# Performer layer and eight-expert MLP on one core: the eighth expert's bias added to its rows before the products, the seventh's rows finished tile by tile, and three tiles' logit steps of the last batch on GpSimd

## The chip, the cores and the metric

One Trainium2 chip, one core. The metric is the device time of one execution of the whole program in microseconds (us), given as the median of several runs. The engines are named as the profile names them: PE is TensorE (matmuls), PEld its weight loads, DVE is VectorE, ACT is ScalarE, POOL is GpSimd, SP is SyncE, which only issues DMAs. PSUM is the memory that matmuls write to, SBUF the memory that all engines read and write.

## The reference, cut to what matters

The input is 8 x 512 tokens of 256 numbers. Each token passes a layer of linear attention with an MLP, then a mixture of 8 experts. In the second part each expert takes the 512 tokens with the highest gate score for it (so a token can have several experts, or none), and adds its weighted output to those tokens.

```python
def ffn(x):                       # x: 4096 rows of 256
    scores = softmax(x @ gate_w.T)            # 8 experts
    vals, idx = top_k(scores.T, 512)          # for each expert: its 512 rows
    y = layernorm(x[idx]) * ln_w + ln_b
    h = gelu(y @ fc1s[e] + b1s[e])            # 1024 hidden
    out = (h @ fc2s[e] + b2s[e]) * vals       # bias b2s, then the weight
    return x.at[idx].add(out)                 # added to the rows

x = x + layernorm(attention_layer(layernorm(x)))
x = x + layernorm(ffn(layernorm(x)))
```

All is float32. A token's result is final when every expert that chose it has added its output; then the row is normalised once more, added to the row that the first part gave (the residual), and written to the output.

## The kernel before, in words

**Two stages with a search between them.** The first stage runs over 8 batches of 512 tokens, each of 4 tiles of 128 tokens (one token per partition). It computes attention and MLP, three layernorms one after the other (letters c, d and e in the code) and, beside them, the gate logits. The logits aren't computed from the finished row: they are carried along as 8 extra columns of the tile `r1x` (columns D to D + E), and each layernorm's effect on them is made up for by small steps on 8 numbers per token: subtract the mean times a constant row, multiply by the root, add another row. `share` (line 486) does this on VectorE, one tile at a time, in one operation or two (L488, L490); `shares` (line 471) does it on GpSimd, in two operations or four (L478, L479, L481, L482). In batches 0 to 6 GpSimd does it for all four tiles at once. In the last batch (`last_mlp`, line 1155) VectorE does it tile by tile, inside the steps `second`, `third` and `fourth` of each tile (lines 1261 to 1281).

The square root of a layernorm, `root` (line 156), is on GpSimd: add epsilon (L157), raise to -0.5 (L158). So each tile of the last batch goes VectorE, GpSimd, VectorE, GpSimd, and so on: step 1 on VectorE (task `("L", b, t, 1)`: take the MLP's product out of PSUM, L1254; mean and variance, `stats`, L153 and L154; first half of the affine map, L1258), root 1 on GpSimd (`("R", b, t, 1)`), step 2 on VectorE (L183, `stats`, L180 for the centring), root 2, step 3 (L183, `stats`), root 3, step 4 (the bias of the last normalisation, L1278).

When all four tiles' logits are done, `chosen_from` (line 1022) turns them into scores: largest value (L1026), difference (L1028), times the root (L1031), all on VectorE, then the exponential on ScalarE (L1035), then sum, reciprocal and product on VectorE (L1038 to L1041). These are the tasks `("CH", b, 0)` to `("CH", b, 2)`. The search needs the scores of the whole input: about 30 rounds of compare and count on VectorE and TensorE (L1477 to L1489), then the row numbers of each expert, its gather of rows (`y`, L1612) and its first product.

**The experts.** For each expert e (0 to 7; the text's "eighth" is e = 7) there are 4 tiles j of 128 rows. TensorE computes the hidden part (`hidden`, L1717) and the second product (`weighted`, L1735), which stays in PSUM. ScalarE takes it out and multiplies it by the token's score (`weighted_out`, L1743, task `We`), VectorE adds the bias times the score (`with_bias`, L1750, task `WB`). For e < 7 GpSimd then issues a DMA that adds the rows to a table in DRAM (`scatter`, L1626, with an addition; task `A1` for the table `accs`). From e = 3 (`L0`) on, the rows' final value is made along the way: before expert e adds, its 512 rows of `accs`, sum and residual, are gathered into `zg` (`gather_sum`, L1612, task `Q`), VectorE adds the expert's own output there (`sum_rows`, L1784, task `U`), takes mean and variance (`told`, task `RS`), GpSimd the root (`RR`), VectorE normalises and adds the residual, and GpSimd scatters the rows to the output (task `P`, L1626 without addition). A later expert that has some of the same tokens writes them again, so the scatters of expert e follow those of e - 1. For e = 3 to 6 mean, root, normalisation and residual are done for the four tiles together: `told` for 4, one `root` on 4 columns, four `applied` (L161), one `with_residual` over 1024 columns (L1775), and only then the four scatters. For e = 7 they are done tile by tile: `RS`, `RR`, and `finish_row` (L161 through `plain`, then L1790).

**What sets the order.** Each engine works through its own queue in program order, and the program order is made on the host by a planner (line 187). Every piece of work is a task with an engine, a cost, a place and the tasks that it must follow. The planner keeps a clock for each engine; it takes, for the engine that can start first, the task with the lowest place among those that can start by then (within 0.05). So costs and places change the order of instructions in a queue, and nothing else: a task with a low place goes ahead of others only if the planner thinks that it is ready. The places of the first stage get 66 for each batch. Those of the experts get 31 for each expert (`SPAN`), through the local function `task` (line 1796). The tasks with a DMA behind them (gathers, scatters, weight loads) are added by `landed` (line 1664), which calls the planner's `add` directly with the place that it is given.

GpSimd's queue holds, in the expert stage, the roots, all gathers and all scatters; each gather or scatter holds the engine for 1.0 to 1.7 us while it makes the descriptors (L1612, L1626), and each scatter has a tiny memset ahead of it (L1625).

## Time and profile before

| | us |
|---|---|
| median of 3 runs | 895.32 (892.78 to 896.16) |
| profiled execution, its own time | 894.79 |
| its span, first to last instruction | 893.1 |
| TensorE busy | 787.7 (88%) |
| VectorE busy | 594.5 (67%) |
| ScalarE busy | 352.6 (39%) |
| GpSimd busy | 344.8 (39%) |
| last matmul of the last batch (L1242) ends | 579.7 |
| exponential of the last batch's scores (L1035) starts | 590.72 |
| first gather of the experts (L1612) starts | 633.64 |
| last product of the eighth expert taken out of PSUM (L1743) starts | 875.82 |
| last scatter (L1626) starts | 885.00 |

How to read it: the span is counted from the first instruction, and all times below are positions on it. Busy shares are means over stages that differ: TensorE is nearly idle from 580 to 638 and after 876, and without rest between. A line of the timeline gives start, duration, engine, source line, operation, what it writes and reads, and in brackets how long the engine was idle before it and which instruction's end released it.

### The profile page before, as it was taken

What the parts mean: (1) busy time and instruction counts of PE and PEld (TensorE: products, weight loads), DVE (VectorE), ACT (ScalarE), POOL (GpSimd) and SP (SyncE); (2) the same over time, 40 slices, a digit from 0 to 9 for tenths busy, and PEclk for the clock granted to TensorE, in tenths of its full rate; (3) what the DMA queues carried; (4) which work ended last, traced back from release to release, by engine and by line L of the source; (5) the groups of instructions that cost most, each with busy time, mean ns of one, the idle gap of its engine ahead of it and who ended that gap; (6) DMA issues with size and microseconds to landing.
All of it is one profiled execution on the core that took longest, in us unless ns stands there. A gap on an engine that the chain in (4) does not pass through costs nothing.

```text
span 893.1 us, 14823 instructions
## 1 busy us (share of the span) xinstructions
PE 787.7 (88%) x5620; PEld 552.1 (62%) x5620; DVE 594.5 (67%) x1631; ACT 352.6 (39%) x638; POOL 344.8 (39%) x548
## 2 busy tenths in 40 slices
PE   4998899999999989999989999911599999999992
PEld 2675585575586666576577578801385676667761
DVE  4568658688677788787877876887553112977223
ACT  3461624454464364463464463300233223322230
POOL 5077103313203213302312302640156766766775
PEclk9998999999999999999999999955599999999996
DMA  9000001301300400400210300174036659987541
GB/s 309 2 2 1 1 1 36 107 3 43 100 1 1 142 3 1 142 2 2 93 51 1 119 2 1 48 241 184 25 103 147 123 116 324 268 284 226 161 95 47
DMA packets 62231, 79.46 MB, mean 89 GB/s; under 512 B 8016, under 2 KB 52304, under 8 KB 62032
## 3 DMA queue, kind: packets, MB, share of 16 engines
q1 hardware_dynamic: 51600, 60.18, 20.3%
q0 software_dynamic: 9856, 17.46, 8.9%
q8 instruction: 44, 0.72, 0.3%
q10 hardware_dynamic: 704, 0.88, 0.3%
q14 instruction: 27, 0.22, 0.1%
HBM read 45.33 MB, written 33.18 MB: 88 GB/s over the span
## 4 chain that ended last, share of the span: by engine, by line
PE 44%; DVE 23%; POOL 12%; issue 12%; DMA 7%; ACT 2%; POOLq 0%; SPq 0%; ACTq 0%; DVEq 0%
PE pm L1004 7%; PE ph L951 6%; PE ptq L833 3%; PE pc L744 3%; PE pv L688 3%; DMA z<-acc 3%; POOL accs L1626 2%; PE pw L932 2%; PE pk L564 2%; PE pq L564 2%; DVE qd L814 2%; DVE sh L807 2%; PE phe L1717 2%; PE pdiv L864 2%; PE pxk L627 2%
## 5 line engine op out<-in xcount | busy, mean ns | idle before, releaser
L951 PE MATMUL ph<-xaT,w_sb 128*128 128x512 f32 (+1 forms) x288 | 118.3, 553 | 0.4 <-ACT hT L956 0.4
L1717 PE MATMUL phe<-yT,w1e 128*128 128x512 f32 (+1 forms) x288 | 115.2, 555 | 0.2 <-ACT yT L1707 0.2
L1735 PE MATMUL pwe<-w2e,hTe 128*128 128x256 f32 x512 | 112.7, 380 | 0.0
L1004 PE MATMUL pm<-w_sb,hT 128*128 128x264 f32 x448 | 107.6, 389 | 0.0
L1735 PEld LDWEIGHTS pwe<-w2e,hTe 128*128 128x128 f32 x512 | 96.5, 190 | 13.5 <-issue 0.5
L1004 PEld LDWEIGHTS pm<-w_sb,hT 128*128 128x128 f32 x448 | 82.3, 190 | 15.5 <-issue 2.8
L1717 PEld LDWEIGHTS phe<-yT,w1e 128*128 128x128 f32 x288 | 54.9, 194 | 51.8 <-issue 48.8
L951 PEld LDWEIGHTS ph<-xaT,w_sb 128*128 128x128 f32 x288 | 53.4, 191 | 48.1 <-issue 36.6
L956 ACT ACTIVATE hT<-ph,cols_sb 128x512 f32<-128x512 f32 (+1 forms) x72 | 45.7, 637 | 68.3 <-PE ph L951 68.3
L1726 ACT ACTIVATE hTe<-phe,cols_sb 128x512 f32<-128x512 f32 (+1 forms) x72 | 45.9, 640 | 66.8 <-PE phe L1717 65.7
L724 ACT ACTIVATE kp<-kp,nstab 128x256 f32<-128x256 f32 x128 | 53.5, 495 | 32.8 <-DVE nstab L677 32.8
L1612 POOL DMA_INDIRECT y<-xg,idx x32 | 33.8, 1056 | 68.3 <-DVE idx L1609 40.0
L1626 POOL DMA_INDIRECT accs<-o,idx x28 | 47.1, 1681 | 16.1 <-issue 10.1
L646 DVE TENSOR_REDUCE mxk<-pxk 128x8 f32<-128x512 f32 x64 | 43.7, 683 | 7.0 <-PE pxk L627 7.0
L1743 ACT ACTIVATE o<-pwe,gg 128x256 f32<-128x256 f32 x32 | 15.1, 473 | 83.7 <-PE pwe L1735 73.0
L807 DVE TENSOR_REDUCE sh<-pxq 128x8 f32<-128x512 f32 x64 | 40.9, 681 | 9.8 <-PE pxq L627 9.7
L814 DVE TENSOR_TENSOR qd<-pxq,sh 128x512 f32<-128x512 f32 x64 | 43.0, 687 | 2.6 <-PE ptq L833 0.5
L649 DVE TENSOR_TENSOR kp<-pxk,diag 128x512 f32<-128x512 f32 x64 | 43.7, 683 | 0.0
L844 ACT ACTIVATE qpT<-ptq 128x512 f32<-128x512 f32 x64 | 35.1, 595 | 19.7 <-PE ptq L833 19.4
L744 PE MATMUL pc<-kp,v_aug 128*34 128x128 f32 x512 | 36.9, 294 | 5.7 <-DVE kp L730 5.7
L833 PE MATMUL ptq<-ident,qd 128*128 128x128 f32 x256 | 35.4, 278 | 5.1 <-ACT qd L826 4.3
L157 POOL TENSOR_SCALAR rs_b<-mv_b 128x4 f32<-128x4 f32 (+1 forms) x9 | 2.4, 269 | 91.9 <-DVE mv_b L154 91.9
(273 smaller groups left out, 1525.0 us busy)
## 6 DMA issues: line engine op xcount, KB each, us to landing
w1e<-in_f SPq DMA_DIRECT2D x8, 1024.0 KB, 6.4
w2e<-in_f SPq DMA_DIRECT2D x8, 1024.0 KB, 8.9
z<-acc SPq DMA_DIRECT2D x8, 1024.0 KB
x<-in_x_in SPq DMA_DIRECT2D x8, 512.0 KB, 9.3
accs<-x SPq DMA_DIRECT2D x8, 512.0 KB, 3.1
acc<-x SPq DMA_DIRECT2D x8, 512.0 KB, 4.3
xg<-xf SPq DMA_DIRECT2D x8, 512.0 KB, 4.3
accs<-xf SPq DMA_DIRECT2D x8, 512.0 KB, 4.2
```

What stands on the lines that cost most here:

```text
L724: nc.scalar.activation(kp[:, :, h, :], kp[:, :, h, :], AF.Exp, bias=nstab[:, h : h + 1])
L744: nc.tensor.matmul(pc[s * 64 : s * 64 + 2 * (DH + 1), i, :], v_aug[:, t, pair, :].rearrange("p h d -> p (h d)"), kp[:, t, pair, :].rearran ...
L807: nc.vector.tensor_reduce(head_cols(kept["sh", b, t], i), pxs[:, :, i, :, :], AX.X, ALU.max,)
L814: nc.vector.tensor_tensor(heads(get("qd", u), c), pxs[:, :, c, :, :], head_cols(kept["sh", b, t], c) .unsqueeze(3).to_broadcast([P, 4, 2, M]),
L833: nc.tensor.transpose(pt[:, i, :], get("qd", u)[:, 2 * hp : 2 * hp + 2, :].rearrange("p h m -> p (h m)"), ident,)
L951: nc.tensor.matmul(ph, w1_sb[:, c, ts(f, P)], get("xaT", b)[:, c, cols], start=(c == 0), stop=(c == KD - 1),)
L956: nc.scalar.activation(get("hT", b)[:, f, cols], ph, AF.Relu, bias=cols_sb[:, C_B1 + f : C_B1 + f + 1])
L1004: nc.tensor.matmul(kept["PM", b, t, 0], get("hT", b)[:, f, ts(t, P)], w2_sb[:, f, :], start=(f == 0), stop=(f == NF - 1),)
L1626: this = nc.gpsimd.indirect_dma_start(out=table[:, :], out_offset=bass.IndirectOffsetOnAxis(ap=idxs[e][:, j : j + 1], axis=0), in_=src, in ...
L1717: nc.tensor.matmul(ph, w1e[:, c, ts(f, P)], yT[:, c, cols], start=(c == 0), stop=(c == KD - 1))
L1726: nc.scalar.activation(hTs[e][:, f, cols], kept["H", e, f, i], AF.Gelu_apprx_tanh, bias=cols_sb[:, col : col + 1],)
L1735: nc.tensor.matmul(kept["W", e, j], hTs[e][:, f, ts(j, P)], ws[e][1][:, f, :], start=(f == 0), stop=(f == NF - 1),)
```

## The change

It has three parts.

1. **Eighth expert.** ScalarE's pass over the product and VectorE's `with_bias` are left out for e = 7. The bias times the score is added to the gathered rows as soon as they are there (`bias_to_rows`, task `UB`), and the product goes from PSUM, times the score, into the same rows in one VectorE operation (`last_sum`, task `U`).
2. **Seventh expert.** The four `applied` and the one `with_residual` become four `finish_row`, one for each tile, and each tile's scatter follows its own row. The places of mean, root, rows and scatters are lower. The cost that the planner is given for the eighth's roots goes from 0.8 to 1.6.
3. **Last batch.** For tiles 0 to 2 the logit steps leave VectorE's steps and become tasks of their own on GpSimd (`LG`), by `shares` on one tile; those of tile 2 are told to follow roots of tile 3. For the last tile they stay on VectorE, and its last one moves from step 4 into step 3. `chosen_from` is cut once more, between the difference and the product with the root, so that largest value and difference wait for the logits only.

```diff
-        def chosen_from(b, pl, rs):
+        def chosen_from(b, pl, rs, early=False):
...
+            if early:
+                yield
             nc.vector.tensor_tensor(
                 ex, ex, rs.unsqueeze(2).to_broadcast([P, NT, E]), ALU.mult
             )
...
+            def to_logits(t, letter, i, plus=None):
+                (mv, rs), x = one(letter, t), in_r1(b)
+                if t == NT - 1:
+                    share(x[:, t, :], mv[:, 0, 0:1], i, rs if plus is not None else None, plus)
+                else:
...
+                    shares(
+                        nc.gpsimd, x[:, t : t + 1, :], mv[:, :, 0], i,
+                        rs if plus is not None else None, plus,
+                    )
+            def logits_2(t):
+                to_logits(t, "c", ns3, k3)
+            def logits_3(t):
+                to_logits(t, "d", ns1, note("x0g", b, None)[:, t, :])
+            def logits_4(t):
+                to_logits(t, "e", ns1)
...
-                    share(in_r1(b)[:, t, :], one("c", t)[0][:, 0, 0:1], ns3, one("c", t)[1], k3)
+                    if t == NT - 1:
+                        logits_2(t)
...
-                    share(
-                        in_r1(b)[:, t, :], one("d", t)[0][:, 0, 0:1], ns1, one("d", t)[1],
-                        note("x0g", b, None)[:, t, :],
-                    )
+                    if t == NT - 1:
+                        logits_3(t)
+                        logits_4(t)
...
-                    share(in_r1(b)[:, t, :], mv[:, 0, 0:1], ns1)
...
-                    (1, 1.48, first, "c"), (2, 1.75, second, "d"), (3, 1.4, third, "e"),
-                    (4, 0.34, fourth, None),
+                    (1, 1.48, first, "c"), (2, 1.75 if last else 1.3, second, "d"),
+                    (3, 1.65 if last else 1.1, third, "e"), (4, 0.16, fourth, None),
...
+                if not last:
+                    for step, weight, work in (
+                        (2, 1.0, logits_2), (3, 1.0, logits_3), (4, 0.5, logits_4)
+                    ):
+                        task(
+                            ("LG", b, t, step), "POOL", weight, at_ + 6 + 2.5 * step,
+                            lambda t=t, work=work: work(t),
+                            [("L", b, t, step - 1)]
+                            + ([("R", b, t, step - 1)] if step < 4 else [])
+                            + ([("LG", b, t, step - 1)] if step > 2 else [])
+                            + ([("R", b, t + 1, min(step - 1, 2))] if t == NT - 2 else []),
+                        )
...
-            for i, (engine, weight) in enumerate((("DVE", 0.57), ("ACT", 0.23), ("DVE", 0.53))):
...
+                (("DVE", 0.38), ("DVE", 0.19), ("ACT", 0.23), ("DVE", 0.53))
...
+                    ("CH", b, i), engine, weight, 82 + 0.1 * i, lambda i=i: chosen(i),
+                    [("CH", b, i - 1)] + ([("R", b, t, 3) for t in range(NT)] if i == 1 else [])
+                    if i else [("LG", b, t, 4) for t in range(NT - 1)] + [("L", b, NT - 1, 3)],
...
+    def bias_to_rows(e, j):
+        zj = zgs[e][:, j, 0:D]
+        nc.vector.scalar_tensor_tensor(
+            zj, b2s_sb[:, e, :], ggs[e][:, j : j + 1], zj, ALU.mult, ALU.add
+        )
+
+    def last_sum(e, j):
+        zj = zgs[e][:, j, 0:D]
+        nc.vector.scalar_tensor_tensor(
+            zj, kept["W", e, j], ggs[e][:, j : j + 1], zj, ALU.mult, ALU.add
+        )
...
+            if e == E - 1:
+                continue
             task(
                 ("We", e, j), "ACT", 0.48, 18.7 + 3.6 * j, lambda e=e, j=j: weighted_out(e, j),
...
+                task(
+                    ("UB", e, j), "DVE", 0.49, 10 + 3.6 * j, lambda e=e, j=j: bias_to_rows(e, j),
+                    [("Q", e, j), ("K", e)],
+                )
+                task(
+                    ("U", e, j), "DVE", 0.49, 18.7 + 3.6 * j, lambda e=e, j=j: last_sum(e, j),
+                    [("UB", e, j), ("W", e, j, 1)], back=("W", e, j, 0),
+                )
...
-                    ("RR", e, j), "POOL", 0.8, 21.5 + 3.6 * j,
+                    ("RR", e, j), "POOL", 1.6, 21.5 + 3.6 * j,
...
-            late = 32 if e < E - 2 else 31
+            late = 32 if e < E - 2 else 26
...
+            if e == E - 2:
+                for j in J:
+                    task(
+                        ("RX", e, j), "DVE", 0.84, late + 3.5 + 0.5 * j,
+                        lambda e=e, j=j: finish_row(e, j), [("RW", e)],
+                    )
...
-                ("P", e, j), "POOL", 1.4, ((late + 10) if e < E - 1 else 25) + 2 * j,
+                ("P", e, j), "POOL", 1.4, ((late + (10 if e < E - 2 else 4)) if e < E - 1 else 25) + 2 * j,
                 lambda e=e, j=j: scatter(out, e, j, zgs[e][:, j, 0:D]),
-                [("RX", e, j) if e == E - 1 else ("RX", e)]
+                [("RX", e, j) if e >= E - 2 else ("RX", e)]
```

## The prediction

> **What bounds the kernel now.** I read the busy shares of the page first, then busy time by stage (the windows view), then the chain of waits, then the two ends that the change touches, row by row on the timeline. In the windows view the columns are stage, length, then each engine's busy time, granted clock, DMA share and GB/s.
>
> ```profile
> 563.00:577.00 14.00, 14.00 (x65) 11.99 (x64) 13.10 (x48) 4.87 (x10) 6.20 (x13) 1.00 0.21 72
> 577.00:592.00 15.00, 2.91 (x14) 2.20 (x14) 11.87 (x47) 3.62 (x8) 11.55 (x27) 0.66 0.50 166
> 640.00:860.00 220.00, 220.00 (x1030) 150.54 (x1031) 103.50 (x274) 71.29 (x123) 144.59 (x170) 0.99 0.67 182
> 876.00:886.00 10.00, 0.00 (x0) 0.00 (x0) 6.08 (x16) 0.30 (x1) 6.71 (x14) 0.64 0.11 39
> ```
>
> From 640 to 860 TensorE is busy all 220.00 us and nothing in the change touches it. The change can act in two places: the end of the last batch (577 to 592), where VectorE and GpSimd hand a chain to and fro while TensorE idles, and the tail after the last product (876 on). Whatever the first place wins passes whole to the end: from the scores on, the chain is the search on VectorE (592 to 633), then the gathers, then the unbroken TensorE stretch. The first place ends like this:
>
> ```profile
> 587.57 0.48 DVE L183 SCALAR_TENSOR_TENSOR x<-r1x,rs_d,x 128x256 f32<-128x256 f32 x1
> ...
> 588.81 0.22 POOL L157 TENSOR_SCALAR rs_e<-mv_e 128x1 f32<-128x1 f32 x1 [0.70 <-DVE mv_e L154]
> ...
> 589.12 0.57 POOL L158 TENSOR_TENSOR rs_e<-rs_e,mhalf 128x1 f32<-128x1 f32 x1
> ...
> 589.72 0.16 DVE L1278 SCALAR_TENSOR_TENSOR nbe<-mv_e,rs_e 128x1 f32<-128x1 f32 x1 [0.62 <-POOL rs_e L158]
> ...
> 590.50 0.19 DVE L1031 TENSOR_TENSOR ex<-ex,rs_e 128x32 f32<-128x32 f32 x1
> ...
> 590.72 0.23 ACT L1035 ACTIVATE ex<-ex 128x32 f32<-128x32 f32 x1 [0.20 <-DVE ex L1031]
> ```
>
> The last root ends at 589.69; five small VectorE steps stand between it and the exponential at 590.72. The tail, GpSimd and the VectorE steps that it waits for:
>
> ```profile
> 864.51 1.01 POOL L1612 DMA_INDIRECT zg<-accs,idx  x1 [0.30 <-issue]
> ...
> 865.89 1.04 POOL L158 TENSOR_TENSOR rs_r<-rs_r,mhalf 128x4 f32<-128x4 f32 x1
> ...
> 866.97 1.38 DVE L161 TENSOR_SCALAR zg<-zg,mv_r,rs_r 128x256 f32<-128x256 f32 x4 [15.11 <-POOL rs_r L158]
> 868.38 1.23 DVE L1775 TENSOR_TENSOR zg<-zg 128x1024 f32<-128x1024 f32 x1
> ...
> 869.90 1.11 POOL L1626 DMA_INDIRECT out<-zg,idx  x1 [2.91 <-DVE zg L1775]
> ...
> 873.96 0.97 POOL L1626 DMA_INDIRECT out<-zg,idx  x1 [0.22 <-issue]
> 874.96 0.26 POOL L157 TENSOR_SCALAR rs_r<-mv_r 128x1 f32<-128x1 f32 x1
> ...
> 881.77 1.09 POOL L1626 DMA_INDIRECT out<-zg,idx  x1 [1.14 <-DVE zg L1790]
> ...
> 885.00 1.09 POOL L1626 DMA_INDIRECT out<-zg,idx  x1 [1.15 <-DVE zg L1790]
> ```
>
> From 865 GpSimd's queue sets the end, not the products: the root of the seventh expert, a wait of 2.91 for its rows, its four scatters, and only then the roots of the eighth (874.96), though the first products were ready at 865.4. After the last scatter (886.09) comes only its landing, to 893.1.
>
> **The tail, part by part.** I call the experts 6 and 7, as the code does. Does the root of expert 6 move ahead of the gathers, as its earlier place (26 for 31) might suggest? Its mean was ready at 851.86 and it still ran at 865.55. The reason is in the code: names added through `landed` carry no offset of their expert, so gathers and scatters have places from -24 to 48, while a root of expert 6 has 186 + 28 = 214. A ready scatter or gather always wins. So the order stays: scatters of 5, gathers of 7, root of 6 at 865.55. What changes is what follows. Rows leave tile by tile: scale 0.41 and residual 0.43 (L161, L1790) with a gap of 0.04 end at 866.97 + 0.88 = 867.85, in place of 869.61; the scatter starts 0.29 later, as now: 868.14 for 869.90, **1.76 earlier**. The other three follow at GpSimd's pace (4.06 for the three), slower than VectorE's 0.88 a tile.
>
> Expert 7's bias step (0.48) moves ahead of the products and the ACT pass (0.47), bias (0.48) and add (0.42) become one operation from PSUM; no row has that form, the nearest are 0.43 (L1254, PSUM and SBUF) and 0.48 (L1750): 0.45, and between 0.4 and 0.6 nothing hangs on it. It frees about 0.9 us of latency per tile. What hides that is GpSimd: by hand through the new order on VectorE the four means are ready at 872.6, 873.8, 877.1 and 880.4, and GpSimd comes to their roots at 873.2, 874.1, 877.9 and 881.1. From the first root on GpSimd's string (root, root, scatter, scatter, root, scatter, root, scatter; places 25 to 31 for the scatters, 238 and more for the roots) is the one of now, with its waits for root, row and scatter; it ran from 874.96 to 885.00 and starts 1.76 earlier. Were that cover gone, the last tile alone would give 875.8 + 0.5 + 0.6 + 0.95 + 0.9 + 0.3 = 879.1. **The tail: -1.76.** New waits: the bias steps of tiles 0 and 1 stand on VectorE ahead of the rows of 6 and wait for the gathers of 7, the second of which is issued by 862.89, 4.08 before VectorE is wanted.
>
> **The last batch.** VectorE loses, for three tiles, small steps of 0.40, 0.37 and 0.14 by their pitch (L488, L490), 2.7 us in all; the last tile keeps them. GpSimd gains, per tile, two steps of four operations and one of two, on 128x8. No row has 8 wide. Nearest: 128x16, shortest 0.21, gap 0.08: 4 x 0.29 = 1.16. Above: the means of the 32-wide rows, 0.34 + 0.38 + 0.31 + 0.41 and four gaps, 1.76, waits within the operations included. I take 1.35, nearer the narrow one (two operations: 0.62, ends 0.58 and 0.88). A root of one tile takes 0.88 where undisturbed (579.16 to 580.04) and 1.05 on the mean of the twelve: 0.95.
>
> Then the order by the planner's rule (first ready, among those the lowest place). With the added steps GpSimd no longer rests: from the second root of tile 0 (ready 566.6, as now) I find no wait over 0.2 down to the last root. In order: that root, step 2 of tile 0's logits, root 1 of tile 1, root 3 of tile 0, and so on; batch 6's root, its logits and its rescale; then roots of tiles 2 and 3 with tile 2's steps among them, and the last step and batch 6's copy ahead of the last root. The sum: 11 roots x 0.95 = 10.45; 5 four-operation steps x 1.35 = 6.75; 3 of two x 0.62 = 1.86; batch 6: root 1.33, logits 0.71, rescale 2.02, copy 0.42, 4.48. Together 23.54, so the last root ends at 590.15, **0.46 later** than now. VectorE falls out as the bound: its stretch to 576.89 ends about 1.7 sooner, and the last product (579.66) now waits for nobody. Behind the root stand no longer five steps but one: largest value and difference move ahead of it, so the exponential starts 0.06 + 0.20 + 0.03 = 0.29 after it in place of 1.03: 590.44 for 590.72. **-0.3.** Ends of this term: roots 0.89 and steps 1.16 / 0.58 with 0.3 of waits for VectorE give 589.0, -1.7; roots 1.05 and steps 1.76 / 0.88 give 566.6 + 27.5 + 0.29 = 594.4, +3.7.
>
> The waits within GpSimd's operations can be seen:
>
> ```profile
> 583.11 0.48 DVE L1258 SCALAR_TENSOR_TENSOR r1x<-r1x,mv_c,rows_sb 128x256 f32<-128x256 f32 x1
> 583.16 0.51 POOL L157 TENSOR_SCALAR rs_c<-mv_c 128x1 f32<-128x1 f32 x1 [0.23 <-DVE mv_c L154]
> ```
>
> The same GpSimd operation took 0.22 at 582.06, beside a VectorE add that reads PSUM (581.97); here it ends 0.08 after the VectorE step does. The Trainium skill ("SBUF — State Buffer", section "SBUF: two separate sides") says why: the two engines share a pair of ports, a VectorE operation with two SBUF inputs takes it whole against a GpSimd operation that reads SBUF, and who starts second waits. It speaks against moving small steps to GpSimd; the row agrees. By that rule alone, each step caught once (+0.29), the string would be 8 x 0.29 = 2.3 longer than undisturbed steps; by no lock, 1.16 a step.
>
> **The sum.** -0.3 - 1.76 = -2.0 on the profiled execution's 894.79 (span 893.1): **892.8 us**. It lies 0.5 below the median of the runs shown (895.32).
>
> **Rivals.**
> 1. GpSimd's string in the last batch stretches (the slower side). Place: between 566.6 and the last root; price up to +3.7, so 894.79 + 3.7 - 1.8 = 896.7. It decides once the string is 2.0 longer than 23.54, that is a four-operation step of 1.67. For it: no rest is left in the queue, and 0.22 became 0.51 above. Against it: VectorE has less to do there. The Trainium skill's rule of the shared port (same page and section) is this rival's mechanism. Chance 0.2.
> 2. The planner gives GpSimd the last root ahead of the third scatter of expert 7. Then the root's 0.9 and the wait for the rows lie beside the scatter: last scatter at 881.4, the tail -3.6; with the undisturbed steps 894.79 - 1.7 - 3.6 = 889.5, with mine 890.9. For it: the eighth's rows are ready sooner. Against: that scatter's place is 29, and it is ready as soon as its row is. Chance 0.15, of which 0.1 below 890.3.
> 3. The bias steps at the head of VectorE's queue hold back the rows of 6: it takes a gather's landing of over 4.08 (a gather of y landed in 2.85, a scatter with addition in up to 6.73). At 6.73 the rows start 3.1 later, tail +1.4: 895.9. Chance 0.05.
> 4. The change does nothing that counts: string and tail as now, 894.8. Chance 0.05.
>
> The forecast has 0.51 (its own range 891.3 to 894.5); 0.04 is left for what I have not seen. The range that should hold the time 8 times in 10: **890.6 to 896.0**. About 0.5% (4.5 us) is what a measurement of this kernel can tell from no change. Faster by more: 0.1 (rival 2). Slower by more needs 899.3, beyond every end above: the 0.04 left over. Within: 0.86.
>
> **What would show it.** In the profile after: the root of expert 6 behind the four gathers of 7, its first scatter 1.2 after that root's end (2.97 now), the eighth's first root right behind the fourth scatter; the gap from first root to last scatter unchanged at 10.04. In the last batch: GpSimd without rests of over 0.3 from 567 on, the exponential 0.3 behind the last root. Wrong would be: roots of 7 waiting for means rather than for GpSimd, rests on GpSimd before the last root, or the last root before 589.

## The result, and the profile after

| | before | after |
|---|---|---|
| median of 9 runs each, side by side | 895.32 (892.78 to 899.20) | 890.64 (887.87 to 892.04) |
| profiled execution, its own time / span | 894.79 / 893.1 | 887.87 / 886.2 |

The ratio is 0.9942, 95% interval [0.9926, 0.9959]. By this ratio the change saves 5.2 us (the two medians are 4.7 apart), where 2.0 were forecast. The sign and the tail were right, the size was not.

The two profiles are 6.9 us apart, but not all of that is the change. The second root of the last batch's first tile starts at 566.64 before and at 564.50 after, so 2.14 us lay between the two executions already. (The first moved step runs ahead of it, in time in which GpSimd was idle before; the tile's first root, ahead of every moved step, lies 2.16 apart.) I therefore compare stretches, each from its own start:

| us | before | after | difference |
|---|---|---|---|
| second root of tile 0 to the end of the last root | 23.05 | 21.92 | -1.13 |
| last root's end to the exponential | 1.03 | 0.29 | -0.74 |
| exponential to the experts' first gather | 42.92 | 42.61 | -0.31 |
| expert 6's first scatter into `accs` to the last scatter | 37.30 | 35.65 | -1.65 |
| sum | | | -3.83 |

The 0.95 still missing to 6.9 lies in TensorE's unbroken stretch, from the first gather to that scatter into `accs` (214.06 before, 213.11 after).

The windows of after, with the columns of before (stage, length, PE, PEld, DVE, ACT, POOL, granted clock, DMA share, GB/s):

```profile
563.00:577.00 14.00, 14.00 (x66) 12.03 (x65) 11.78 (x39) 5.89 (x13) 11.07 (x37) 1.00 0.23 77
577.00:592.00 15.00, 1.69 (x8) 0.90 (x7) 12.30 (x50) 2.47 (x7) 12.07 (x31) 0.59 0.68 219
640.00:855.00 215.00, 215.00 (x1014) 146.63 (x1013) 100.18 (x267) 68.19 (x117) 144.13 (x170) 1.00 0.69 186
871.00:880.00 9.00, 0.00 (x0) 0.00 (x0) 3.39 (x10) 0.00 (x0) 5.44 (x11) 0.62 0.16 55
```

In the first row GpSimd has gone from 13 operations and 6.20 to 37 and 11.07, VectorE from 48 to 39 operations; part of that is that after runs 2.14 ahead in the same window. The third row is TensorE's unbroken work, as before. Now GpSimd's timeline in the last batch; an operation's share of the queue is read from its start to the next start:

```profile
564.50 0.39 POOL L157 TENSOR_SCALAR rs_d<-mv_d 128x1 f32<-128x1 f32 x1 [0.70 <-DVE mv_d L154]
...
568.57 0.20 POOL L478 TENSOR_TENSOR gm<-mv_c,gk 128x8 f32<-128x8 f32 x1
568.85 0.20 POOL L479 TENSOR_TENSOR r1x<-r1x,gm 128x8 f32<-128x8 f32 x1
569.13 0.20 POOL L481 TENSOR_TENSOR r1x<-r1x,rs_c 128x8 f32<-128x8 f32 x1
569.41 0.28 POOL L482 TENSOR_TENSOR r1x<-r1x,gk 128x8 f32<-128x8 f32 x1
569.65 0.20 POOL L478 TENSOR_TENSOR gm<-mv_e,gk 128x8 f32<-128x8 f32 x1
569.93 0.20 POOL L479 TENSOR_TENSOR r1x<-r1x,gm 128x8 f32<-128x8 f32 x1
570.10 0.22 POOL L157 TENSOR_SCALAR rs_d<-mv_d 128x1 f32<-128x1 f32 x1
...
572.47 0.22 POOL L157 TENSOR_SCALAR rs_e<-mv_e 128x1 f32<-128x1 f32 x1 [0.43 <-DVE mv_e L154]
...
585.85 0.57 POOL L158 TENSOR_TENSOR rs_e<-rs_e,mhalf 128x1 f32<-128x1 f32 x1
```

A step of four takes 1.08 (568.57 to 569.65), one of two 0.45 (569.65 to 570.10), and the only idle time over 0.3 from there up to the last root is the 0.43 at 572.47 (the next longest is 0.14). The end of the batch over all engines:

```profile
585.97 0.18 DVE L1026 TENSOR_REDUCE lm<-r1x 128x4 f32<-128x32 f32 x1
...
586.19 0.19 DVE L1028 TENSOR_TENSOR ex<-r1x,lm 128x32 f32<-128x32 f32 x1
...
586.48 0.19 DVE L1033 TENSOR_TENSOR ex<-ex,rs_e 128x32 f32<-128x32 f32 x1
...
586.71 0.23 ACT L1037 ACTIVATE ex<-ex 128x32 f32<-128x32 f32 x1
```

The last root ends at 586.42. Largest value and difference run beside it (585.97, 586.19), and one product (L1033, L1031 before) stands between root and exponential. GpSimd in the tail:

```profile
859.22 1.01 POOL L1647 DMA_INDIRECT zg<-accs,idx  x1 [0.31 <-issue]
...
860.76 1.04 POOL L158 TENSOR_TENSOR rs_r<-rs_r,mhalf 128x4 f32<-128x4 f32 x1
...
863.00 1.11 POOL L1661 DMA_INDIRECT out<-zg,idx  x1 [1.14 <-DVE zg L1838]
...
868.07 0.25 POOL L157 TENSOR_SCALAR rs_r<-mv_r 128x1 f32<-128x1 f32 x1
...
874.86 1.09 POOL L1661 DMA_INDIRECT out<-zg,idx  x1 [1.15 <-DVE zg L1838]
...
878.08 1.09 POOL L1661 DMA_INDIRECT out<-zg,idx  x1 [1.15 <-DVE zg L1838]
```

The wait ahead of expert 6's first scatter is 1.14 instead of 2.91; behind it stands the order of before, and from 868.07 to 878.08 it takes 10.01 (10.04 before).

### The profile page after: what moved, and what is told of

Read it like the earlier page. It is cut to its first block, busy times and chain, and to the rows that moved or that the text cites. A ratio compares the mean times of both kernels' runs of the same rounds, so it can differ in the third digit from the quotient of the medians.

```text
span 886.2 us, 14834 instructions
## 1 busy us (share of the span) xinstructions
PE 787.3 (89%) x5620; PEld 552.6 (62%) x5620; DVE 595.1 (67%) x1619; ACT 351.0 (40%) x634; POOL 350.2 (40%) x578
## 4 chain that ended last, share of the span: by engine, by line
PE 68%; DVE 16%; POOL 5%; issue 5%; ACT 3%; DMA 1%; POOLq 0%; ACTq 0%; DVEq 0%
PE phe L1752 11%; PE pwe L1770 11%; PE ph L951 7%; PE pm L1004 7%; PE pc L744 4%; PE ptq L833 3%; PE pv L688 3%; PE pw L932 3%; PE pk L564 2%; PE pq L564 2%; PE pxq L627 2%; PE pdiv L864 2%; PE pxk L627 2%; PE pr L909 2%; PE pm L1262 2%
## 5 line engine op out<-in xcount | busy, mean ns | idle before, releaser
L814 DVE TENSOR_TENSOR qd<-pxq,sh 128x512 f32<-128x512 f32 x64 | 42.9, 686 | 2.6 <-PE ptq L833 0.5
L1778 ACT ACTIVATE o<-pwe,gg 128x256 f32<-128x256 f32 x28 | 13.3, 474 | 75.2 <-PE pwe L1770 75.2
```

## The experiments

Two theories stood against each other. **S**: the sum stands and only the size of GpSimd's string in the last batch was wrong; what is left over separates executions of one kernel. **M**: another stretch, above all the one from the scores to the experts, gains by itself. All ratios are to the kernel before, run beside on the same chip. In the table, "string" runs from the second root of tile 0 to the end of the last root, "behind" from there to the exponential, "search" from the exponential to the experts' first gather, "rows and scatters" from expert 6's first scatter into the output to the last scatter, "tail" from expert 6's first scatter into `accs` to the last scatter.

| | ratio, interval | string | behind | search | rows and scatters | tail |
|---|---|---|---|---|---|---|
| before | 1 | 23.05 | 1.03 | 42.92 | 15.10 | 37.30 |
| after | 0.9942 [0.9926, 0.9959] | 21.92 | 0.29 | 42.61 | 15.08 | 35.65 |
| e1_batch_only | 0.9975 [0.9961, 0.9990] | 21.84 | 0.29 | 42.59 | 15.09 | 37.26 |
| e2_tail_only | 0.9971 [0.9952, 0.9989] | 23.04 | 1.04 | 42.89 | 15.08 | 35.71 |
| e3_rows_only | 1.0008 [0.9988, 1.0027] | 23.03 | 1.03 | 42.89 | 17.29 | 37.69 |
| e4_product_only | 0.9984 [0.9969, 1.0000] | 23.04 | 1.03 | 42.89 | 14.11 | 36.64 |
| e5_split_only | 1.0014 [0.9994, 1.0033] | 23.05 | 0.44 | 43.26 | as before | 37.31 |
| e6_gpsimd_only | 1.0006 [0.9987, 1.0026] | 21.69 | 1.04 | 42.93 | as before | 37.26 |
| e7_two_more | 0.9989 [0.9969, 1.0010] | 23.96 | 0.26 | 42.59 | as after | 35.55 |
| e8_late_rescale | 0.9913 [0.9894, 0.9932] | 21.60 | 0.29 | 43.04 | as after | 35.76 |
| e9_tail_order | 0.9957 [0.9936, 0.9978] | 21.82 | 0.30 | 42.61 | 16.53 | 36.34 |
| e10_both_orders | 0.9967 [0.9952, 0.9982] | 21.74 | 0.29 | 43.06 | 16.41 | 36.21 |
| e11_before_again | 0.9987 [0.9971, 1.0004] | 23.06 | 1.04 | 42.93 | as before | 37.31 |
| e12_products_first | 0.9937 [0.9915, 0.9959] | 21.85 | 0.30 | 42.61 | 13.49 | 33.34 |
| e13_changed_again | 0.9967 [0.9952, 0.9981] | 21.83 | 0.30 | 42.61 | as after | 35.84 |
| e14_late_rescale_again | 0.9967 [0.9953, 0.9980] | 21.75 | 0.29 | 43.04 | as after | 35.71 |

**The two halves.** The change to the last batch alone, and the two parts of the tail alone.

```diff
 # e1_batch_only, against the kernel before: part 3 of the change
+            if early:
+                yield
...
+            def to_logits(t, letter, i, plus=None):
...
+                            ("LG", b, t, step), "POOL", weight, at_ + 6 + 2.5 * step,
```

> Only the last batch's part of the change; the tail is that of before. In the two profiles the exponential of the scores comes 1.85 us sooner when counted from batch 6's first third-normalisation row (561.88 and 559.72), not 0.3 as forecast. Theory S (the sum stands, the GpSimd string was sized too long, and the rest of the gap between the two profiles is chance of the execution): about -1.9 us, ratio 0.998. Theory M (the stretch from the scores to the experts adds a gain of its own, 0.6 in the first matmuls of the first expert and some 0.6 around them): about -3.1 us, ratio 0.9965. In the profile both expect the last root to end about 22 us behind the start of the second root of tile 0 and the exponential 0.29 behind the last root; S expects the first eight matmuls of expert 0 to take 3.1 or 3.7 without regard to the change.

```diff
 # e2_tail_only, against the kernel before: parts 1 and 2 of the change
+                    ("UB", e, j), "DVE", 0.49, 10 + 3.6 * j, lambda e=e, j=j: bias_to_rows(e, j),
...
+                        ("RX", e, j), "DVE", 0.84, late + 3.5 + 0.5 * j,
```

> Only the two expert parts of the change; the last batch is that of before. Theory S: -1.65 us, ratio 0.998, first scatter of the seventh expert's rows 1.2 behind the root's end (2.97 before), and 15.1 from that first scatter to the last, as before. Rival P (the eighth's product leaving by one operation is worth time by itself): more than -1.65, and less than 15.1 between the two scatters.

The last batch alone gives 0.9975, the tail alone 0.9971; their stretches are each as in the whole change (21.84 and 0.29; 35.71), and the rest of each as before. The interval of the first ratio holds what both theories expect (0.998 and 0.9965), so it's the stretches that speak for S. The product of the two ratios is 0.9946, against 0.9942 measured. So there are two parts that add, and no third that needs both has to be assumed. Half of the win, about 2 us, comes from the last batch, which had been forecast at 0.3.

**The tail in its parts.** Only the seventh expert's rows by tile, and only the eighth's products by one operation (with its cost for the planner).

```diff
 # e3_rows_only, against the kernel before
-            late = 32 if e < E - 2 else 31
+            late = 32 if e < E - 2 else 26
...
+                        ("RX", e, j), "DVE", 0.84, late + 3.5 + 0.5 * j,
+                        lambda e=e, j=j: finish_row(e, j), [("RW", e)],
```

> Only the seventh expert's rows by tile, with its new places; the eighth expert is that of before, its roots' planner cost is 0.8 again. The planner now orders GpSimd root 0, scatter 0, root 1, scatter 1, root 2, scatter 2, root 3, scatter 3. Theory S (GpSimd's order and length set the tail): the first scatter of the seventh comes 1.76 sooner, but root 1 stands behind scatter 0, which waits for root and row, so most is given back: about -0.2 us. A theory by which only the seventh's rows matter expects -1.7.

```diff
 # e4_product_only, against the kernel before
+                    ("U", e, j), "DVE", 0.49, 18.7 + 3.6 * j, lambda e=e, j=j: last_sum(e, j),
+                    [("UB", e, j), ("W", e, j, 1)], back=("W", e, j, 0),
...
-                    ("RR", e, j), "POOL", 0.8, 21.5 + 3.6 * j,
+                    ("RR", e, j), "POOL", 1.6, 21.5 + 3.6 * j,
```

> Only the eighth expert's part (bias first, product by one operation, its roots' planner cost 1.6); the seventh's rows are those of before. GpSimd's order becomes root 0, root 1, scatter 0, root 2, scatter 1, scatter 2, root 3, scatter 3. Theory S: the seventh's first scatter stays (2.97 behind the root), root 2 ahead of scatter 1 saves one wait: about -0.9 us. Rival P: -1.5 or more. A theory by which the eighth's part is worth nothing: 0.

With the rows alone, the first scatter is 1.76 earlier (1.21 behind the root's end, 2.97 before), and all of it is given back: rows and scatters take 17.29. GpSimd's timeline of that kernel shows how:

```profile
874.68 1.34 POOL L1626 DMA_INDIRECT out<-zg,idx  x1 [1.34 <-DVE o L1750]
876.05 0.24 POOL L157 TENSOR_SCALAR rs_r<-mv_r 128x1 f32<-128x1 f32 x1
...
878.15 1.09 POOL L1626 DMA_INDIRECT out<-zg,idx  x1 [1.15 <-DVE zg L1790]
...
881.36 1.09 POOL L1626 DMA_INDIRECT out<-zg,idx  x1 [1.15 <-DVE zg L1790]
...
884.58 1.09 POOL L1626 DMA_INDIRECT out<-zg,idx  x1 [1.14 <-DVE zg L1790]
```

Here every scatter of the eighth expert stands right behind its own root and waits 1.14 to 1.34 for VectorE to make the rows from it. Before and after, two of the four stand so; with the product alone, one (its order is root, root, scatter, root, scatter, scatter, root, scatter). In these four kernels the lengths go with that count: 17.29 with four, 15.08 to 15.10 with two, 14.11 with one. The rows by tile alone end at +0.39 in the tail (about -0.2 had been expected), the eighth's part alone at -0.66 (-0.9 expected), and both together at -1.65; whether the operation itself or the root's planner cost of 1.6 sets that order was not run apart.

**The last batch in its parts.** Only the cut of the scores (with the last tile's logits ahead of its root), and only the move to GpSimd.

```diff
 # e5_split_only, against the kernel before: all steps stay on VectorE
+            if early:
+                yield
...
-                    ("CH", b, i), engine, weight, 93 + i, lambda i=i: chosen(i),
+                    ("CH", b, i), engine, weight, 82 + 0.1 * i, lambda i=i: chosen(i),
```

> Only the cut in the scores of the last batch: largest value and difference ahead of the last root, the last tile's last logit step with them; all logit steps stay on VectorE; the tail is that of before. Theory S (GpSimd's and VectorE's order as before, the chain behind the root shorter): from the start of the second root of tile 0 to the last root's end 23.05 as before, the exponential 0.29 behind it for 1.03, so -0.7 us. A theory by which the move to GpSimd alone brings the last batch's gain expects 0.

```diff
 # e6_gpsimd_only, against the kernel before: the scores are not cut
+                            ("LG", b, t, step), "POOL", weight, at_ + 6 + 2.5 * step,
```

> Only the move of three tiles' logit steps to GpSimd; the last tile's steps and the scores stand as before; the tail is that of before. Theory S: the stretch from the second root of tile 0 to the last root's end is 21.9, the exponential 1.03 behind it: -1.1 us, and scores to gather 42.9 or 42.6, which tells whether the 0.3 found there goes with the move. The forecast's size of the string (23.54) would give +0.5.

The cut alone leaves the string at 23.05 and takes 0.59 off what stands behind it (0.74 had been expected); the move alone takes 1.36 off the string and leaves 1.04 behind it. The two add to 1.95, and the whole change has 1.87. The search is no shorter in either (43.26 and 42.93), so its 0.31 doesn't come with the move alone. Neither can be told from no change by its time (1.0014 and 1.0006): effects of this size are seen in the stretches of a profile, not in the ratios.

**Is GpSimd's string the bound?** Two operations more on GpSimd at each moved step (they write spare numbers that nobody reads), and batch 6's rescale taken out of the string, to after the last root.

```diff
 # e7_two_more, against the changed kernel
+                    for n in range(2):
+                        spare = small.tile([P, 1, E], F32, tag="spare", name=f"spare_{t}{letter}{n}")
+                        nc.gpsimd.tensor_tensor(spare, gk[:, 0:1, :], gk[:, 1:2, :], ALU.mult)
```

> The changed kernel with two further GpSimd operations of the same size (128x8, on numbers that nobody reads) in each moved logit step. Theory S (GpSimd's queue is now the bound of the last batch, with under 0.7 of rests in it): 8 of the 9 steps lie within the string, 8 x 2 x 0.28 = 4.5 less the rests, so the last root ends 3.8 to 4.5 later behind the second root of tile 0 (25.7 to 26.4 for 21.92), and the time is 4 us over the changed kernel's, about that of before or 0.5 above. Rival V (the chain of VectorE steps and roots behind the last product is the bound, GpSimd has slack): 1.5 or less.

```diff
 # e8_late_rescale, against the changed kernel
-            task(("SC", b), "POOL", 1.7, at_ + 22, scale, [("eR", b), ("SG", b - 2)])
+            task(("SC", b), "POOL", 1.7, at_ + 22, scale, [("eR", b), ("SG", b - 2)] + ([("R", b + 1, NT - 1, 3)] if b == NB - 2 else []))
```

> The changed kernel with batch 6's rescale (four GpSimd operations, 1.94) told to follow the last root of the last batch. Theory S: the string is shorter by 1.94 until the first root of tile 3 (behind the last product) binds; then that root, 1.1, 0.9, 1.1 and so on: the last root 1.0 sooner (20.9 for 21.92), time -1.0 us against the changed kernel. Rival V: the same or less. If GpSimd's queue does not bind: 0.

The 16 added operations that lie in the string lengthen it by 2.04, less than the 3.8 to 4.5 of S and more than the 1.5 of V. The reason is in their rows (two operations are one row, x2):

```profile
571.56 0.20 POOL L482 TENSOR_TENSOR r1x<-r1x,gk 128x8 f32<-128x8 f32 x1
571.72 0.36 POOL L1251 TENSOR_TENSOR spare_1c<-gk 128x8 f32<-128x8 f32 x2
572.04 0.20 POOL L478 TENSOR_TENSOR gm<-mv_e,gk 128x8 f32<-128x8 f32 x1
```

An operation that needs nothing of the one ahead starts 0.16 behind it (571.56, 571.72), not 0.28, so a pair costs 0.32 and eight pairs 2.6. Of these 2.6, 2.04 reach the end: the string on GpSimd is nearly the bound. Taking 1.94 out of it, however, shortens it by only 0.32, for GpSimd then waits:

```profile
576.82 0.38 POOL L157 TENSOR_SCALAR rs_d<-mv_d 128x1 f32<-128x1 f32 x1 [1.29 <-DVE mv_d L154]
577.04 0.42 DVE L1274 TENSOR_TENSOR r1x<-pm,r1x 128x264 f32<-128x264 f32 x1
577.28 0.57 POOL L158 TENSOR_TENSOR rs_d<-rs_d,mhalf 128x1 f32<-128x1 f32 x1
578.23 0.51 POOL L157 TENSOR_SCALAR rs_c<-mv_c 128x1 f32<-128x1 f32 x1 [0.38 <-DVE mv_c L154]
```

The wait of 1.29 is for the third tile's second mean. VectorE now makes this mean ahead of the last tile's product, and takes that product (577.04) 13.77 behind the second root of tile 0; in after it is 13.12 (577.62). So close behind GpSimd's string stands the exchange of the last two tiles between VectorE and GpSimd, and in this order about 0.3 is left to win on GpSimd. Theory S alone had expected more of both; there are two chains of nearly one length.

**The order in the tail.** Root of expert 6 ahead of the gathers of 7, and the eighth's roots ahead of the scatters of the tile before (their cost for the planner is 0.8 again).

```diff
 # e9_tail_order, against the changed kernel
-                ("Q", e, j), "POOL", 1.4, -2 + 1.5 * j, lambda e=e, j=j: gather_sum(e, j),
+                ("Q", e, j), "POOL", 1.4, (60 if e == E - 1 else -2) + 1.5 * j, lambda e=e, j=j: gather_sum(e, j),
...
-                    ("RR", e, j), "POOL", 1.6, 21.5 + 3.6 * j,
+                    ("RR", e, j), "POOL", 0.8, 21.5 + 3.6 * j,
...
-            task(("RR", e), "POOL", 1.4, late + 2, lambda e=e: root(*lns["r", e], NJ), [("RS", e)])
+            task(("RR", e), "POOL", 1.4, late + 2 - (300 if e == E - 2 else 0), lambda e=e: root(*lns["r", e], NJ), [("RS", e)])
...
-                ("P", e, j), "POOL", 1.4, ((late + (10 if e < E - 2 else 4)) if e < E - 1 else 25) + 2 * j,
+                ("P", e, j), "POOL", 1.4, {E - 2: 70, E - 1: 300}.get(e, late + 10) + 2 * j,
...
+                + ([("RR", e, j + 1)] if e == E - 1 and j < NJ - 1 else [])
```

> The changed kernel with another order on GpSimd in the tail: the seventh expert's root as soon as its mean is there, ahead of the eighth's gathers, the seventh's scatters right behind those, and each of the eighth's scatters behind the next tile's root. Theory S (GpSimd's string sets the tail): the seventh's first scatter follows the last gather with no wait for root and rows, and the last root lies beside the rows of tile 2: from the start of the last gather to the start of the last scatter 15.8 us (18.86 in the changed kernel, 20.49 before), time -3 us against the changed kernel, ratio 0.991 to before. If the eighth's products set the tail, the last scatter could start no sooner than 3.5 behind the last product's end, some 2 us sooner than this.

> The changed kernel with both other orders, the late rescale and the tail's. Theory S: the two gains add, -1.0 and -3.0 against the changed kernel, -8 us against before, ratio 0.991.

(e10 is e9 with e8's edit.) The order was reached, the gain was not: the tail took 36.34, and 36.21 in e10, against 35.65. The last gather to the last scatter had become 1.0 shorter (17.85 for 18.86), but that is no gain: the root of expert 6 (1.4 us) had moved ahead of that start, so the measure was not the same one. GpSimd's row shows the new wait, VectorE's the cause:

```profile
872.40 0.23 POOL L157 TENSOR_SCALAR rs_r<-mv_r 128x1 f32<-128x1 f32 x1 [2.07 <-DVE mv_r L154]
```

```profile
868.06 0.18 DVE L154 BATCH_NORM_AGGREGATE mv_r<-st_r 128x2 f32<-128x6 f32 x1
870.36 0.41 DVE L161 TENSOR_SCALAR zg<-zg,mv_r,rs_r 128x256 f32<-128x256 f32 x1 [2.12 <-POOL rs_r L158]
870.81 0.42 DVE L1838 TENSOR_TENSOR zg<-zg 128x256 f32<-128x256 f32 x1
871.15 0.48 DVE L1830 SCALAR_TENSOR_TENSOR zg<-pwe,gg,zg 128x256 f32<-128x256 f32 x1
```

VectorE idles 2.12 for the first root, because the rows of tile 0 stand ahead of the sum of tile 1 (871.15) in its queue; so the second mean is late, and GpSimd, waiting for it, idles too. The two queues wait for each other in turn. The next kernel lets tile j's rows follow tile j + 1's mean:

```diff
 # e12_products_first, against e9_tail_order
-                    [("RR", e, j)],
+                    [("RR", e, j)] + ([("RS", e, j + 1)] if j < NJ - 1 else []),
...
-                + ([("RR", e, j + 1)] if e == E - 1 and j < NJ - 1 else [])
```

> The tail of the run with the changed GpSimd order (root of expert 6 ahead of its gathers, each root of expert 7 ahead of the scatters that do not need it), but on VectorE the rows of tile j of expert 7 now follow the mean of tile j+1, so that no sum of products waits behind rows. That sum stood 3 us late there and cost two roots their time. Theory S (the tail is GpSimd's queue, and what it saves passes whole to the end): from the last gather of expert 7 to the last scatter about 15.3 us, 18.86 in the changed kernel and 17.85 in that run; the last scatter starts about 3.8 behind the end of the last product; the time about 3.5 below the changed kernel, 7 to 8 below the kernel before, a ratio of about 0.992. The rival (the last product and VectorE's steps behind it set the end as soon as GpSimd has room; the order adds nothing further): the stretch stays at 17.5 or more, the ratio near that run's 0.9957.

```profile
868.82 0.26 POOL L157 TENSOR_SCALAR rs_r<-mv_r 128x1 f32<-128x1 f32 x1
...
869.74 0.21 POOL L157 TENSOR_SCALAR rs_r<-mv_r 128x1 f32<-128x1 f32 x1
...
871.15 1.08 POOL L1661 DMA_INDIRECT out<-zg,idx  x1 [0.49 <-DVE zg L1830]
872.27 0.29 POOL L157 TENSOR_SCALAR rs_r<-mv_r 128x1 f32<-128x1 f32 x1
...
873.45 1.10 POOL L1661 DMA_INDIRECT out<-zg,idx  x1 [0.18 <-DVE st_r L153]
874.58 0.25 POOL L157 TENSOR_SCALAR rs_r<-mv_r 128x1 f32<-128x1 f32 x1
...
875.71 1.18 POOL L1661 DMA_INDIRECT out<-zg,idx  x1 [0.18 <-issue]
...
877.19 0.99 POOL L1661 DMA_INDIRECT out<-zg,idx  x1 [0.21 <-issue]
```

No scatter stands right behind its own root any more, and the longest wait is 0.49. From the last gather it takes 14.81 (15.3 expected), in the tail's own measure 33.34: 2.3 less than after. The changed kernel beside it had a median of 890.30, this one 887.31, the kernel before 893.27: ratio 0.9937. Its stretches give -1.9 - 0.3 - 4.0 = -6.2, its ratio -5.6. The interval of the ratio holds the values of both theories (0.992 and 0.9957); the 14.81, against 17.5 or more, is what decides for S. The last scatter starts 5.2 behind the last product's end (871.95), not 3.8; GpSimd's queue, without a rest of over 0.5, is still the bound. Its tail is the shortest of the study.

**How much is chance.** The kernel before beside itself, and the changed kernel and e8 once more.

> The kernel before, unchanged, timed against itself. It shows what the measurement gives for no change: ratio 1.000 with an interval of some 0.2% to each side; in the profile 24.08 us from the second root of tile 0 to the exponential, 42.9 from there to the first gather, 18.07 from the seventh's root to the last scatter, and first matmuls of expert 0 that take what the clock gives in this execution (3.1 to 3.8).

> The changed kernel, unaltered, beside the kernel before once more. Its three touched stretches are 3.8 us shorter than before, its measured time 5.2 us. Theory S (the touched stretches are the whole effect, the rest is what separates executions of one kernel): a ratio of 0.9950 to 0.9965. The rival (the code's layout or the other clock adds about 1.4 us that the stretches do not show): 0.9935 to 0.9945 again.

> The kernel with the rescale of batch 6 after the last root, unaltered, once more. Its touched stretches were as those of the changed kernel within 0.1 us, yet its time was 3.8 us below it (ratio 0.9913). Theory S (the stretches are the whole effect): 0.995 to 0.9965, with the changed kernel of the same call within 0.001 of it. The rival (the later rescale wins something outside the stretches): 0.991 to 0.9925 again, 0.002 or more below the changed kernel of this call.

Unaltered code gave 0.9987 in e11. The changed kernel gave 0.9967 where it had given 0.9942, and e8 0.9967 where it had given 0.9913. What e8 had won beyond the changed kernel (2.6 us by the ratios, 3.8 by medians that were not taken side by side) didn't come back. No stretch of its profile had shown it: e8's stretches add to -3.6, for -3.83 in after. Its five executions all had a mean granted clock of 0.951 to 0.953, those of before beside them 0.944 to 0.952.

The two series of the changed kernel say 5.2 and 2.9 us less, their middle 4.1, and the stretches 3.8. Theory S holds: no gain outside the stretches is needed. M's place in the experts' first matmuls goes with the execution: the first eight of expert 0 took 3.70 before and 3.10 after, but 3.62 in the changed kernel run again (mean granted clock over the four us around them: 0.55, 0.70 and 0.57). So does the 0.95 of TensorE's unbroken stretch: where after had 213.11, e13 has 215.59.

The edge of S is the search, which is 42.6 in after, e1, e7, e9, e12 and e13 and 42.9 to 43.3 in the others. Before has one longer gap there:

```profile
610.11 0.16 DVE L1489 SCALAR_TENSOR_TENSOR un_l<-ptot_l,eb_l 128x1 f32<-128x1 f32 x1 [0.19 <-PE ptot_l L1482]
...
611.26 0.16 DVE L1489 SCALAR_TENSOR_TENSOR un_l<-ptot_l,eb_l 128x1 f32<-128x1 f32 x1 [0.46 <-PE ptot_l L1482]
```

0.46 where the rounds beside it have 0.19: 0.27 more. After has no such gap in any round. The length goes with the kernel, not with the execution (e11 has 42.93 as before, e13 42.61 as after, e8 and e14 both 43.04). Why one round is longer in before, e2, e3, e4, e6 and e11 is open. In e5, e8, e10 and e14 no round is longer either, and the extra lies ahead of the first round, in VectorE's cast of the scores (tile `kh`, L1489 in after and e8): 0.65 in after, 1.07 in e8, 1.31 in e5. Two GpSimd memsets (L1596 in after and e8) run beside it, and in the ten profiles where the end of one can be read on a row, the cast ends 0.14 to 0.15 behind it. So it looks as if the place of these memsets in GpSimd's order made this difference of up to 0.66; it is read from the rows, and no run here moved the memsets alone.

## Why the prediction was wrong, point by point

**The step that failed is the last batch's term**, -0.3, and in it the size of GpSimd's string: "The sum: 11 roots x 0.95 = 10.45; 5 four-operation steps x 1.35 = 6.75; 3 of two x 0.62 = 1.86; batch 6: ... 4.48. Together 23.54". Measured in after: roots 10.29, steps of four 5.54 (1.01 to 1.27), of two 1.32, batch 6 4.20, and waits 0.57, which the sum did not have: 21.92. The steps alone are 1.75 of the 2.19 that the terms were too high; the waits, which the forecast put at nothing ("no wait over 0.2"), give 0.57 back. The forecast had the undisturbed pitch of the nearest row at hand (128x16: 0.21 and a gap of 0.08, 1.16 for four) and moved away from it toward 32-wide rows, which hold waits of another place. The two whole 128x16 steps in before took 1.57 and 1.55, waits included, so its profile left open how much the moved steps would be held up; the runs showed that they hardly were. 8-wide operations took 0.20 at a pitch of 0.28. With 1.11 and 0.44 for the steps and all else as forecast, the string would have been 21.80 and the term 21.80 + 0.29 - 24.08 = -2.0; measured is -1.87. That this comes so close is partly luck, since the roots and batch 6, 0.44 too high, nearly make up for the missing waits.

Where the forecast drew its line ("the last root before 589" would be wrong) the measurement lies beyond it: 586.42, or 588.56 with the 2.14 by which this execution was ahead. Its sign "without rests of over 0.3" failed too, at the 0.43.

**Right in the last batch**: the order, one step behind the root (0.29 forecast, 0.29 measured), and that VectorE is no longer held up: it now waits 1.03 for the last tile's product (first line below). **Rival 1**, the stretched string, did not come. A row of the kind that spoke for it exists (second line):

```profile
577.62 0.43 DVE L1274 TENSOR_TENSOR r1x<-pm,r1x 128x264 f32<-128x264 f32 x1 [1.03 <-PE pm L1262]
...
578.82 0.52 POOL L157 TENSOR_SCALAR rs_c<-mv_c 128x1 f32<-128x1 f32 x1
```

The root's first operation takes 0.52 where others take 0.22, beside a VectorE step with two SBUF inputs from 578.77 to 579.25; it ends 0.09 behind that step. But over the 26 moved operations of the string all time above 0.20 is 0.48. By the Trainium skill ("SBUF — State Buffer", section "SBUF: two separate sides") the engine that starts second waits for the shared ports; the rule's direction agrees with this row, and the 2.3 that I had worked out from one catch per step is five times what the trace has.

**The tail**, -1.76, was right: root of expert 6 behind the gathers (859.22, then 860.27), first scatter 1.20 behind its end, the eighth's first root right behind the fourth scatter, 10.01 from there to the last. From the end of expert 6's root to the last scatter it takes 16.28 for 18.07. But the reason given ("What hides that is GpSimd") holds for an order that had to be kept: e3 shows the same gain lost whole in another order. **Rival 2** (a root ahead of an earlier scatter) did not come in the changed kernel; e4 shows its like, worth 1.0 in rows and scatters for one root (0.66 over the whole tail). **Rival 3** did not come: the bias steps ran at 858.83 and 860.11, and VectorE still idled 1.24 ahead of the rows at 861.84. **Rival 4** neither: the intervals of both series of the changed kernel lie below 1.

**What else was short.** By the stretches the change saves 3.8, not 2.0: 1.6 more in the last batch, 0.3 in the search, which was not foreseen, and 0.1 less in the tail. The other 1.4 of the 5.2 lie in no stretch that the change touches, and they were not there when the changed kernel was run again (2.9). That the median of 890.64 lies inside the range, by 0.04, is luck: the range's lower end of 890.6 reached toward rival 2, which did not come. The last batch's own lower end (-1.7) together with the tail's -1.76 gives 891.3, and 891.0 with the 0.3 of the search.

## What to carry to other kernels

Where no row has an operation's width, take the undisturbed pitch of the nearest row as one bound and whole steps with their waits as the other, and let the range hold both: here the first was right (1.16 for a measured 1.11). Then count how many operations sit on the queue that ends last. On a queue that issues scatters, a scatter right behind the small operation that its rows depend on costs a round trip to the partner engine each time (here about 1 us); put other ready work between, and order the partner engine's queue so that it doesn't wait for the same thing. Measure a gain below half a per cent by stretches from fixed events, with a start that no edit moves, and run the changed kernel a second time before explaining the rest.

## What the runs showed of the hardware that was not expected

On GpSimd an operation on 128x8 takes 0.20; one that needs the result ahead starts 0.28 behind it, one that doesn't 0.16 (0.14 to 0.17 in after).

Two series of one pair of kernels can differ by more than the intervals of their ratios: 0.9913 [0.9894, 0.9932] in e8 (five executions) and 0.9967 [0.9953, 0.9980] in e14. In the 116 runs of the kernel before that stood beside the experiments, times lie between 889.75 and 900.38, and go with the mean granted clock (0.940 to 0.952): 0.7 us less per 0.001 of clock, correlation -0.88, and alike in each of the four series. Part of that may be the other way round, since the clock is lower where TensorE idles (0.59 from 577 to 592 in after); which drives which is open. In the profiles the untouched stretch from the first hidden product of the experts to expert 7's last gather took 223.80 in one execution of the changed kernel and 226.49 in another (e13).
